# A one-core Perceiver block: softmax weights turned by moves and VectorE, and six steps of a hand-written order placed elsewhere

## The chip, the core and the metric

The kernel runs on one core of a Trainium2 chip. A core has a matrix engine (TensorE, PE in the profile; its weight loads are shown as PEld), a vector engine (VectorE, DVE), an engine for activation functions (ScalarE, ACT), a general engine (GpSimd, POOL) and an engine that here only issues transfers (SyncE, SP; its queue is shown as SPq). Each engine executes its own instructions in order, and they wait for one another by semaphores. Data is worked on in on-chip memory of 128 partitions (SBUF); matrix products land in a second, small memory (PSUM).

The metric is the device time of one execution in microseconds, as the median of several runs.

## What is computed

```python
def reference(x, ctx_1024, ...):
    x = x + _L0_xattn_ref(_layernorm(x), ctx_1024, Wq, bq, Wk, bk, Wv, bv, Wr, br)
    x = x + _L0_attn_ref(_layernorm(x), Wq, Wm, W1, W2, g1, b1, g2, b2)
    x = x + _L0_ffn_ref(_layernorm(x), W, b, ids, weights)

# _L0_xattn_ref: cross attention with cosine features of the keys
    Q, K, V = x @ Wq + bq, y @ Wk + bk, y @ Wv + bv
    K_hat = cos(K @ Wr + br)
    probs = softmax(Q @ K_hat.T)
    return probs @ V
# _L0_attn_ref: linear attention (8 heads) with feat = elu(x @ Wq) + 1, then an MLP
    msg = (feat @ (feat.T @ q) / (feat @ sum(feat))) @ Wm
    x = x + layernorm(msg) * g1 + b1
    x = x + layernorm(relu(msg @ W1) @ W2) * g2 + b2
# _L0_ffn_ref: eight of 32 adapters, summed with weights
    out = x @ sum_k(weights[k] * W[ids[k]]).T + sum_k(weights[k] * b[ids[k]])
```

x is [32, 32, 512] (32 batches of 32 rows), the context y is [32, 257, 512], all in float32. W1 is 512x1024, W2 is 1024x512.

## The kernel before

**Groups.** Four batches of 32 rows make a group of 128 rows, one for each partition; there are eight groups (`NG` = 8), g = 0 to 7. The first half of the groups is 0 to 3.

**The order is written out by hand.** The program is a loop over twelve windows `w` of eight units `u` (L1394 to L1420). In each unit first the steps filed with `ahead` for this place are issued, then the unit's own matrix work, then the steps filed with `at`. A "slot" is 8w + u. Since each engine works in order, this listing is the order on every engine. Within one place, steps stand in the order in which they were filed.

- Windows 0 to 7 make the key features of two batches per four units: `pair_unit`, seven products P1 to P7 of four 128x256 matmuls each (L533), by a scheme that forms sums of blocks first. `ORDER` (L568) is its listing: T1 to T4 are the block sums on VectorE (L521 to L527), C11, C22, C12 and C21 take a product out of PSUM (C22 and C12 are L550 on VectorE, p1, u1, p5 and C21 run on ScalarE, L545), w11 and so on round (ScalarE, L553), f11 and so on take the fraction (VectorE, L557 and L558), S is the sine. A and B turn the next context tiles (L391) and start a later load. P4 adds to the PSUM tile that C22 reads first, and it needs T4; P6 needs T2.
- Windows 8 and 10 are the first MLP product of the first and second half of the groups (`hidden_unit`), by the same scheme with m2 in the place of the context; windows 9 and 11 are the second MLP product (`mlp_unit`).

**A group's steps.** `q_stats`, `q_norm`, `q_turn`, `q_times` make the query; `a_scores` the scores and exp; `a_turn_p` turns the softmax weights p; `a_sum` multiplies them with the plain context (`av`, L828); `a_turn`, `a_values`, `a_norm`, `b_turn`, `b_q`, ... go on to the linear attention; `b_merge` gives m2, `b_turn_m2` writes it turned into `m2T[half]`, from which `m2_sum` makes the block sums t1, t2 and t4 for P5, P6 and P4 of `hidden_unit`. `mlp_stats` and `mlp_norm` norm the MLP's rows; `f_stats`, `f_norm`, `f_turn`, `f_times` are the adapter product. The adapters themselves are summed by 16 `adapter_add` (L718), moved by `adapter_move` and turned by `adapter_turn` into `wff`.

**Two ways to turn a tile.** `turn` (L254) transposes 128x128 blocks on TensorE into PSUM and copies them out. `move` and `turn_moved` (L270, L281) move four blocks of columns with four transfers on SP's queue to 32 partitions each, and transpose 32x32 blocks on VectorE (L283). `a_turn_p` turns p with two TensorE transposes (L817) and a ScalarE copy (L819), behind the unit of step 3; the other turns of groups 0 to 6 are moves. Group 7 (`late`) turns everything on TensorE.

**What shares an engine.** `ln_stats` uses VectorE for statistics and GpSimd for the power (L246, L248); `add_bv` (L761), `mlp_norm` of groups 0 to 3 (L1230, L1231), `f_bias` (L1249) and the sum of two bias rows (L1425) are 128x512 operations on GpSimd.

The lines that file the steps which the change touches:

```python
u = 8 * g + 8 if g < NG - 1 else 8 * g + 4              # q_turn, q_times
steps = {a_scores: 2, a_turn_p: 3, a_sum: 5, ...}       # at
first = {a_turn: 7, a_norm: 9, b_turn: 10, ...}         # ahead
at(0, 4, add_bv, 0)
ahead_slot(slots["add0"] + m, adapter_add, m)
at_slot(slots["m2"], b_turn_m2, NG - 1)                 # slot 79
at_slot(slots["v3" if n else "v1"], m2_sum, 1, i)       # slot 79
```

Of the kernel before, what the change touches and what calls it, by code (L numbers as in the profile page):

```python
# [9 lines left out]
F32 = mybir.dt.float32  # L10
# [16 lines left out]
def tile_perceiver_block(  # L27
# [242 lines left out]
    def move(src, name):  # L270


        m = tmp.tile([P, 4, P], F32, tag="moved", name=f"moved_{name}", bufs=4)
        for q in range(4):
            nc.sync.dma_start(
                out=m[q * 32 : (q + 1) * 32, :, :].rearrange("k n f -> k (n f)"),
                in_=src[:, q * P : (q + 1) * P],
            )
        return m

# [6 lines left out]

    def rows_times(ps, srcT, w):

        n = srcT.shape[1]  # L290
        for c in range(n):
            nc.tensor.matmul(  # L292
                ps, lhsT=srcT[:, c, :], rhs=w[:, c, :], start=(c == 0), stop=(c == n - 1)
            )
# [222 lines left out]

    def block_sum(y11, y12, y21, y22, i):
        t1, t2, t4 = pair_tiles["sums"]
        if i == 1:  # L520
            nc.vector.tensor_tensor(t1, y12, y11, ALU.subtract)  # L521
        elif i == 2:
            nc.vector.tensor_tensor(t2, y22, t1, ALU.subtract)
        elif i == 3:
            nc.vector.tensor_tensor(y12, y22, y12, ALU.subtract)
        else:
            nc.vector.tensor_tensor(t4, y21, t2, ALU.subtract)  # L527
# [264 lines left out]
    def a_scores(g):  # L792
# [17 lines left out]
        nc.vector.reciprocal(rden, den)  # L810
        held["p", g], held["rden", g] = p, rden

    def a_turn_p(g):
        p = held["p", g]
        ps = tr_tile(f"tr_p_{g}")
        for c in range(2):
            nc.tensor.transpose(ps[:, c, :], p[:, c:K0:2], ident)  # L817
        pT = one.tile([P, 2, P], F32, tag="pT", name=f"pT_{g}")
        nc.scalar.copy(pT, ps[:, :2, :])  # L819
        held["pT", g] = pT  # L820
# [222 lines left out]

    def m2_sum(half, i):
        (y11, y12), (y21, y22) = m2_blocks(half)
        block_sum(y11, y12, y21, y22, i)

# [3 lines left out]
    def hidden_unit(half, k, u):  # L1051
# [24 lines left out]
        if u == 0:  # L1076
            product(a, w11, y11, stop=False)
            product(c, w12, y21)
            nc.scalar.copy(part[0], a)
        elif u == 1:  # L1080
            product(a, s2, t2, start=False, stop=False)
            product(d, s1, t1, stop=False)
            add(h[0][0], c, part[0])
            nc.scalar.copy(part[1], a)
            nc.scalar.copy(part[2], d)
        elif u == 2:
            product(a, s3, y12, start=False, stop=False)
# [176 lines left out]

    def f_rows(g, i=0):
        cols = f_parts(g)[i]
# [4 lines left out]
        ff_ps[g, i] = ps[:, : cols.stop - cols.start]  # L1271
        rows_times(ff_ps[g, i], held["h2T", g], ad["wff"][:, :, cols])

# [32 lines left out]

    slots = dict(load3=67, add0=66, wff=83, n=79, f=84, fT=88, ft=89, w1=71, w3=73, w2=66, s0=61, s1=66, t1=63, t3=64, m2=79, v1=79, v3=79, bias=66, h1=72, h2=72, h3=73)
    last = (64, 65, 66, 67, 68, 69, 70, 71, 73, 74, 75, 76, 77, 78, 85, 88)
    six = dict(b_q=10, b_pairs=13, b_msg=14, b_merge=18, b_feat=11, b_turn_f=13, b_turn_msg=16, b_turn_m2=21, b_stats=20, b_norm=21)

    for g in range(NG):
# [3 lines left out]
        if g:  # L1315
            u = 8 * g if g < NG - 1 else 8 * g - 4
            ahead(u // 8, u % 8, q_stats, g)
            ahead((u + 5) // 8, (u + 5) % 8, q_norm, g)
        u = 8 * g + 8 if g < NG - 1 else 8 * g + 4
        ahead(u // 8, u % 8, q_turn, g)  # L1320
        at(u // 8, u % 8, q_times, g)
        w = g + 1
        if g == NG - 1:
# [5 lines left out]
            continue  # L1329
        steps = {a_scores: 2, a_turn_p: 3, a_sum: 5, a_values: 8, b_q: 11, b_pairs: 15, b_msg: 17, b_merge: 22}  # L1330
        first = {a_turn: 7, a_norm: 9, b_turn: 10, b_feat: 13, b_turn_f: 14, b_turn_msg: 20, b_stats: 23, b_norm: 26, b_turn_m2: 31}
        if g == NG - 2:
# [4 lines left out]
        for f, u in first.items():  # L1337
            ahead(w + u // 8, u % 8, f, g)
    at(0, 4, add_bv, 0)
    at(6, 4, adapter_fetch)  # L1340
# [3 lines left out]
    for m in range(2 * NK):  # L1344
        at_slot((59, 60, 63)[m] if m < 3 else slots["load3"] + m - 3, adapter_load, m)
        ahead_slot(slots["add0"] + m, adapter_add, m)
    for c in range(OP):
# [11 lines left out]
    at_slot(slots["ft"] + 1, f_times, 1)  # L1359
    at_slot(slots["m2"], b_turn_m2, NG - 1)  # L1360
    at_slot(68, second_homes)
# [26 lines left out]
    for i in range(1, 5):  # L1388
# [3 lines left out]
        at_slot(slots["t3" if n else "t1"], m2_sum, 0, i)  # L1392
        at_slot(slots["v3" if n else "v1"], m2_sum, 1, i)
    for w in range(12):  # L1394
        for u in range(8):
# [25 lines left out]
            if (w, u) == (0, 2):  # L1421
                add_r = load_row("add_r", b1)
                b2_r = row_tile("b2_r")
                nc.gpsimd.dma_start(out=b2_r, in_=b2.partition_broadcast(P))
                nc.gpsimd.tensor_tensor(add_r, add_r, b2_r, ALU.add)  # L1425
            if (w, u) == (2, 0):
# [19 lines left out]
    f_bias(5)  # L1446
    f_turn(6)
    f_rows(5)
    f_bias(6)
# [61 lines left out]
```

## Time and profile before

| what | value |
|---|---|
| runs before | median 520.6 us of 3 (519.8 to 521.55) |
| the profiled execution | 521.03 us, of it a span of 519.2 us from its first to its last instruction |
| instructions | 9195 |
| granted TensorE clock | 1.000 |
| TensorE / weight loads busy | 511.3 us / 374.2 us |
| VectorE, ScalarE, GpSimd busy | 382.6, 243.9, 164.7 us |
| transfers | 74.64 MB, mean 144 GB/s |
| 436 to 449 us of the span (window 10 begins) | TensorE 11.85, VectorE 12.55, ScalarE 6.41, GpSimd 10.12 us busy in 13.00 |
| 493 to 509 us | TensorE 15.23, VectorE 13.32, GpSimd 6.70 us busy in 16.00 |

The window of group g's scores begins about 44.5 us after that of group g - 1; the eight `a_scores` products start at 65.8, 101.3, 143.5, 188.0, 232.6, 277.2, 321.7 and 358.2 us. A line of the timeline gives start and duration in us, engine, source line, operation, the tiles written and read with partitions x elements, a count, and in brackets the idle time of that engine before it with what ended it. The waits list gives who waited for whom. The chain of waits is followed back from the last instruction.

### The profile page before, as it was taken

What the parts mean: (1) busy time and instruction counts of PE and PEld (TensorE: products, weight loads), DVE (VectorE), ACT (ScalarE), POOL (GpSimd) and SP (SyncE); (2) the same over time, 40 slices, a digit from 0 to 9 for tenths busy, and PEclk for the clock granted to TensorE, in tenths of its full rate; (3) what the DMA queues carried; (4) which work ended last, traced back from release to release, by engine and by line L of the source; (5) the groups of instructions that cost most, each with busy time, mean ns of one, the idle gap of its engine ahead of it and who ended that gap; (6) DMA issues with size and microseconds to landing.
All of it is one profiled execution on the core that took longest, in us unless ns stands there. A gap on an engine that the chain in (4) does not pass through costs nothing.

```text
span 519.2 us, 9195 instructions
## 1 busy us (share of the span) xinstructions
PE 511.3 (98%) x3413; PEld 374.2 (72%) x3413; DVE 382.6 (74%) x645; ACT 243.9 (47%) x465; POOL 164.7 (32%) x202
## 2 busy tenths in 40 slices
PE   8999999999999999999999999999999999999997
PEld 6588977777866767687676778866576786886844
DVE  1398877787886978878779778667476977875593
ACT  1145684485474467348446646735332222451131
POOL 0012110500501340250144316203415836973134
PEclk9999999999999999999999999999999999999999
DMA  8759987655455547824544372535344433211013
GB/s 206 165 126 214 276 181 222 169 151 165 149 168 153 160 124 176 240 77 136 166 146 138 98 228 63 164 103 189 127 152 163 161 101 126 77 56 52 20 41 123
DMA packets 84517, 74.64 MB, mean 144 GB/s; under 512 B 7972, under 2 KB 70448, under 8 KB 84472
## 3 DMA queue, kind: packets, MB, share of 16 engines
q1 hardware_dynamic: 81312, 64.19, 44.6%
q0 software_dynamic: 2864, 9.73, 6.1%
q8 instruction: 27, 0.44, 0.4%
q14 instruction: 18, 0.15, 0.1%
q10 hardware_dynamic: 296, 0.14, 0.1%
HBM read 58.03 MB, written 2.10 MB: 116 GB/s over the span
## 4 chain that ended last, share of the span: by engine, by line
PE 88%; DVE 5%; DMA 2%; POOL 2%; issue 1%; ACT 1%; SPq 1%; POOLq 0%; DVEq 0%; ACTq 0%
PE a L533 20%; PE b L533 9%; PE q L779 6%; PE bq L292 5%; PE xa L292 5%; PE c L533 5%; PE m L292 5%; PE hid_a L533 5%; PE ff L292 3%; PE wkr L324 3%; PE av L828 3%; PE mlp_a L1169 3%; PE sc L797 3%; PE mlp_b L1169 2%; PE hid_b L533 2%; PE z L429 2%
## 5 line engine op out<-in xcount | busy, mean ns | idle before, releaser
L557 DVE SCALAR_TENSOR_TENSOR kh<-parts,kh 128x512 f32<-128x512 f32 x60 | 42.7, 712 | 24.9 <-ACT parts L553 24.9
L553 ACT ACTIVATE parts<-kh,rounder 128x512 f32<-128x512 f32 x60 | 43.2, 720 | 35.8 <-DVE kh L550 35.3
L566 ACT ACTIVATE kh<-kh 128x512 f32<-128x512 f32 x60 | 36.3, 628 | 34.9 <-DVE kh L558 34.6
L246 POOL TENSOR_TENSOR rstd_n<-ve_n,mhalf 128x1 f32<-128x1 f32 x16 | 12.1, 758 | 97.8 <-DVE ve_n L244 96.7
L391 DVE STREAM_TRANSPOSE yT<-quads 128x1024 f32<-128x1024 f32 x31 | 38.2, 1234 | 2.2 <-DMA quads<-in_ctx_dram 2.2
L558 DVE TENSOR_SCALAR kh<-kh 128x512 f32<-128x512 f32 x60 | 31.5, 524 | 2.1
L246 POOL TENSOR_TENSOR rstd_x<-ve_x,mhalf 128x1 f32<-128x1 f32 x8 | 7.7, 962 | 77.8 <-DVE ve_x L244 77.8
L779 PEld LDWEIGHTS q<-hT,wq_sb 128*128 128x128 f32 x256 | 29.8, 192 | 3.1 <-issue 2.6
L533 PE MATMUL a<-sums,wkr 128*128 128x256 f32 x120 | 29.2, 386 | 1.7 <-DVE kh L550 1.7
L779 PE MATMUL q<-hT,wq_sb 128*128 128x128 f32 x256 | 29.9, 275 | 0.0
L533 PE MATMUL a<-yT,m2T 128*128 128x256 f32 x120 | 29.6, 389 | 0.0
L533 PEld LDWEIGHTS a<-sums,wkr 128*128 128x128 f32 x120 | 22.1, 190 | 9.9 <-issue 4.0
L761 POOL TENSOR_TENSOR x<-x,bv_r 128x512 f32<-128x512 f32 x8 | 10.7, 1331 | 57.6 <-ACT h L252 57.6
L533 PE MATMUL a<-yT,wkr 128*128 128x256 f32 x120 | 28.9, 384 | 0.0
L292 PE MATMUL ff<-awq_sb,h2T 128*128 128x512 f32 (+2 forms) x80 | 28.6, 508 | 0.2 <-DVE h2T L283 0.2
L292 PE MATMUL xa<-wv_sb,aoT 128*128 128x512 f32 x64 | 28.8, 592 | 0.0
L292 PE MATMUL bq<-awq_sb,bhT 128*128 128x512 f32 x64 | 28.8, 592 | 0.0
L292 PE MATMUL m<-awm_sb,msgT 128*128 128x512 f32 x64 | 28.8, 592 | 0.0
L533 PE MATMUL a<-sums,m2T 128*128 128x256 f32 x120 | 28.4, 379 | 0.0
L533 PE MATMUL c<-yT,wkr 128*128 128x256 f32 x120 | 28.3, 379 | 0.0
L533 PE MATMUL b<-sums,m2T 128*128 128x256 f32 x120 | 28.3, 379 | 0.0
L533 PE MATMUL b<-yT,m2T 128*128 128x256 f32 x120 | 28.3, 379 | 0.0
(274 smaller groups left out, 1138.8 us busy)
## 6 DMA issues: line engine op xcount, KB each, us to landing
quads<-in_ctx_dram SPq DMA_DIRECT2D x128, 128.0 KB, 3.1
plain<-in_ctx_dram SPq DMA_DIRECT2D x32, 512.0 KB, 5.5
moved_h<-h SPq DMA_DIRECT2D x56, 64.0 KB, 2.2
x<-in_x_dram SPq DMA_DIRECT2D x8, 256.0 KB, 4.4
last<-in_ctx_dram SPq DMA_DIRECT2D x32, 64.0 KB, 2.2
w<-in_L_attn_W_dram SPq DMA_DIRECT2D x4, 512.0 KB, 4.5
moved_ao<-ao SPq DMA_DIRECT2D x28, 64.0 KB, 2.2
moved_bh<-bh SPq DMA_DIRECT2D x28, 64.0 KB, 2.2
```

What stands on the lines that cost most here:

```text
L246: nc.gpsimd.tensor_tensor(rstd, ve, mhalf, ALU.pow)
L292: nc.tensor.matmul(ps, lhsT=srcT[:, c, :], rhs=w[:, c, :], start=(c == 0), stop=(c == n - 1))
L324: nc.tensor.matmul(acc[c], lhsT=wkT[:, e, c * P : (c + 1) * P], rhs=wr_sb[:, e, :], start=(e == 0), stop=(e == DC - 1),)
L391: nc.vector.transpose(t.rearrange("p c (n k) -> p n c k", k=32), quads.pop(b))
L533: nc.tensor.matmul(ps[:, o, :], lhsT=w[:, c, o * P : (o + 1) * P], rhs=yb[:, c, :], start=start and o == 0 and c == 0, stop=stop and o == ...
L553: nc.scalar.activation(w, u, AF.Identity, bias=rounder)
L557: nc.vector.scalar_tensor_tensor(u, w, ROUNDER, u, ALU.subtract, ALU.subtract)
L558: nc.vector.tensor_scalar(u, u, -0.5, 0.5, ALU.max, ALU.min)
L566: nc.scalar.activation(u, u, AF.Sin, scale=-TURN)
L779: nc.tensor.matmul(ps[:, e, :], lhsT=wq_sb[:, d, e * P : (e + 1) * P], rhs=hT[:, d, :], start=(d == 0), stop=(d == DC - 1),)
L797: nc.tensor.matmul(sc[js, :], lhsT=qT[g][:, r, js], rhs=kh[g * GB + j][:, r, :], start=(r == 0), stop=(r == DC - 1),)
L1169: nc.tensor.matmul(ps[:, o, :], lhsT=a[n // 2][:, n % 2, o * P : (o + 1) * P], rhs=b[n // 2][:, n % 2, :], start=start and o == 0 and n == ...
```

## The change

1. `a_turn_p` of groups 0 to 6: `a_scores` now moves the first 256 columns of p with four transfers (`move` takes any width), and `a_turn_p` is one VectorE transpose from the moved tile; it is filed ahead of step 5 and not behind step 3. Group 7 keeps the TensorE way.
2. `add_bv(0)` goes from place (0, 4) to (1, 0), the sum of the two bias rows from (0, 2) to (0, 6); `q_turn` and `q_times` of group 0 go one unit later; `b_turn` of group 0 is filed behind its unit's own work and not ahead of it.
3. `b_turn_m2(7)` goes from behind slot 79 into slot 80, between the first and the second product. The sums t1 and t2 of the second half are made in two column halves: groups 4 and 6 at slot 79, groups 5 and 7 behind `b_turn_m2(7)`. The other two sums (`v3`) go to slot 80.
4. The last two `adapter_add` go one slot later. `mlp_stats` and `mlp_norm` of groups 0 to 3 go two slots later, `f_stats`, `f_norm`, `f_turn` and `f_times` (of 0 and 1) one.
5. In the tail, `f_turn(6)` stands between the first and the second matmul of `f_rows(5)`, and not in front of them.

```diff
     def move(src, name):
-        m = tmp.tile([P, 4, P], F32, tag="moved", name=f"moved_{name}", bufs=4)
+        n = src.shape[1] // 4
+        m = tmp.tile([P, 4 * n], F32, tag="moved", name=f"moved_{name}", bufs=4)
         for q in range(4):
             nc.sync.dma_start(
-                out=m[q * 32 : (q + 1) * 32, :, :].rearrange("k n f -> k (n f)"),
-                in_=src[:, q * P : (q + 1) * P],
+                out=m[q * 32 : (q + 1) * 32, :], in_=src[:, q * n : (q + 1) * n]
             )
-        return m
+        return m.rearrange("p (n f) -> p n f", n=4)
...
-    def rows_times(ps, srcT, w):
+    def rows_times(ps, srcT, w, between=None):
         n = srcT.shape[1]
         for c in range(n):
+            if c == 1 and between:
+                between()
...
-    def block_sum(y11, y12, y21, y22, i):
-        t1, t2, t4 = pair_tiles["sums"]
+    def block_sum(y11, y12, y21, y22, i, cols=slice(0, 2 * P)):
+        y11, y12, y21, y22, t1, t2, t4 = (
+            t[:, :, cols] for t in (y11, y12, y21, y22, *pair_tiles["sums"])
+        )
...
         held["p", g], held["rden", g] = p, rden
+        if not late(g):
+            held["pm", g] = move(p[:, :K0], f"p_{g}")

     def a_turn_p(g):
-        p = held["p", g]
-        ps = tr_tile(f"tr_p_{g}")
-        for c in range(2):
-            nc.tensor.transpose(ps[:, c, :], p[:, c:K0:2], ident)
         pT = one.tile([P, 2, P], F32, tag="pT", name=f"pT_{g}")
-        nc.scalar.copy(pT, ps[:, :2, :])
+        if late(g):
+            p = held["p", g]
+            ps = tr_tile(f"tr_p_{g}")
+            for c in range(2):
+                nc.tensor.transpose(ps[:, c, :], p[:, c:K0:2], ident)
+            nc.scalar.copy(pT, ps[:, :2, :])
+        else:
+            nc.vector.transpose(
+                pT.rearrange("p c (k n) -> p n c k", n=4),
+                held.pop(("pm", g)).rearrange("p n (i c) -> p n c i", c=2),
+            )
         held["pT", g] = pT
...
         if u == 0:
             product(a, w11, y11, stop=False)
+            if (half, k) == (1, 0):
+                b_turn_m2(NG - 1)
+                m2_sum(1, 1, slice(P, 2 * P))
+                m2_sum(1, 2, slice(P, 2 * P))
             product(c, w12, y21)
             nc.scalar.copy(part[0], a)
...
-    slots = dict(..., n=79, f=84, fT=88, ft=89, ..., v1=79, v3=79, ...)
+    slots = dict(..., n=81, f=85, fT=89, ft=90, ..., v1=79, v3=80, ...)
...
-        u = 8 * g + 8 if g < NG - 1 else 8 * g + 4
+        u = 8 * g + (8 if g < NG - 1 else 4) + (g == 0)
...
-        steps = {a_scores: 2, a_turn_p: 3, a_sum: 5, ...}
-        first = {a_turn: 7, ...}
+        steps = {a_scores: 2, a_sum: 5, ...}
+        first = {a_turn_p: 5, a_turn: 7, ...}
...
         for f, u in first.items():
-            ahead(w + u // 8, u % 8, f, g)
-    at(0, 4, add_bv, 0)
+            (at if g == 0 and f == b_turn else ahead)(w + u // 8, u % 8, f, g)
+    at(1, 0, add_bv, 0)
...
-        ahead_slot(slots["add0"] + m, adapter_add, m)
+        ahead_slot(slots["add0"] + m + (m >= 2 * NK - 2), adapter_add, m)
...
-    at_slot(slots["m2"], b_turn_m2, NG - 1)
...
-        at_slot(slots["v3" if n else "v1"], m2_sum, 1, i)
+        if n:
+            at_slot(slots["v3"], m2_sum, 1, i)
+        else:
+            at_slot(slots["v1"], m2_sum, 1, i, slice(0, P))
...
+            if (w, u) == (0, 6):
                 nc.gpsimd.tensor_tensor(add_r, add_r, b2_r, ALU.add)
...
-    f_turn(6)
-    f_rows(5)
+    f_rows(5, between=lambda: f_turn(6))
```

More of the change, by code (lines that the diff above doesn't have):

```diff
@@ L1042, in m2_blocks, with m2_sum @@
         ]
-    def m2_sum(half, i):
+    def m2_sum(half, i, cols=slice(0, 2 * P)):
         (y11, y12), (y21, y22) = m2_blocks(half)
-        block_sum(y11, y12, y21, y22, i)
+        block_sum(y11, y12, y21, y22, i, cols)
     def hidden_tile(half, i):
@@ L1263, in f_parts, with f_rows @@
         return last if g == NG - 1 else (slice(0, D),)
-    def f_rows(g, i=0):
+    def f_rows(g, i=0, between=None):
         cols = f_parts(g)[i]
@@ L1271, in f_rows @@
         ff_ps[g, i] = ps[:, : cols.stop - cols.start]
-        rows_times(ff_ps[g, i], held["h2T", g], ad["wff"][:, :, cols])
+        rows_times(ff_ps[g, i], held["h2T", g], ad["wff"][:, :, cols], between)
     def f_out(g, i=0):
@@ L1305, in ahead_slot @@
         ahead(n // 8, n % 8, *args)
-    slots = dict(load3=67, add0=66, wff=83, n=79, f=84, fT=88, ft=89, w1=71, w3=73, w2=66, s0=61, s1=66, t1=63, t3=64, m2=79, v1=79, v3=79, bias=66, h1=72, h2=72, h3=73)
+    slots = dict(load3=67, add0=66, wff=83, n=81, f=85, fT=89, ft=90, w1=71, w3=73, w2=66, s0=61, s1=66, t1=63, t3=64, m2=79, v1=79, v3=80, bias=66, h1=72, h2=72, h3=73)
     last = (64, 65, 66, 67, 68, 69, 70, 71, 73, 74, 75, 76, 77, 78, 85, 88)
@@ L1329, in tile_perceiver_block @@
             continue
-        steps = {a_scores: 2, a_turn_p: 3, a_sum: 5, a_values: 8, b_q: 11, b_pairs: 15, b_msg: 17, b_merge: 22}
-        first = {a_turn: 7, a_norm: 9, b_turn: 10, b_feat: 13, b_turn_f: 14, b_turn_msg: 20, b_stats: 23, b_norm: 26, b_turn_m2: 31}
+        steps = {a_scores: 2, a_sum: 5, a_values: 8, b_q: 11, b_pairs: 15, b_msg: 17, b_merge: 22}
+        first = {a_turn_p: 5, a_turn: 7, a_norm: 9, b_turn: 10, b_feat: 13, b_turn_f: 14, b_turn_msg: 20, b_stats: 23, b_norm: 26, b_turn_m2: 31}
         if g == NG - 2:
```

## The prediction

> **What bounds the kernel now.** I read first the page's busy times, then what TensorE waited for in the whole run, then the chain of waits and the timelines around each stall.
>
> ```profile
> PE 511.3 (98%) x3413; PEld 374.2 (72%) x3413; DVE 382.6 (74%) x645; ACT 243.9 (47%) x465; POOL 164.7 (32%) x202
> ...
> PE 88%; DVE 5%; DMA 2%; POOL 2%; issue 1%; ACT 1%; SPq 1%; POOLq 0%; DVEq 0%; ACTq 0%
> ```
>
> TensorE is busy for 98% of the span and carries 88% of the chain, at a granted clock of 1.0 throughout. So a microsecond is won only by taking work off TensorE or by closing one of its gaps. This is the complete list of its gaps with a releaser (line, releaser: us in total, times, longest):
>
> ```profile
> PE a L533 <- DVE kh L550: 1.7, 2, 1.0
> PE idle L308 <- POOL ident masks.py:199: 1.4, 1, 1.4
> PE tr_m L258 <- ACT m2s L969: 0.7, 1, 0.7
> PE tr_h L258 <- ACT h L252: 0.6, 1, 0.6
> PE hid_a L533 <- DVE hid L1073: 0.4, 1, 0.4
> PE ff L292 <- DVE h2T L283: 0.2, 1, 0.2
> ```
>
> Without the start-up (L308) that is 3.6 us. The change touches the place of each of them except the last.
>
> **A. Softmax weights turned without TensorE.** For groups 0 to 6 two transposes a group leave TensorE (group 7 keeps them). Their price is the hole that they leave in the chain of waits between bq and the next product:
>
> ```profile
> 191.84 3.43 PE bq L292 x8
> ...
> 195.51 1.73 PE a L533 x8
> ```
>
> bq ends at 195.27, the product starts at 195.51: 0.24 us. The same reading gives 0.23 or 0.24 in each of the seven groups: 7 x 0.235 = 1.65 us won. ScalarE loses seven copies of 0.38, which end nothing. Added are, per group, four 32 KB moves on SP's queue and one VectorE transpose of 128x256 in front of T3. No row shows either. I bound the transpose from below by a quarter of the 128x1024 one (1.24/4 = 0.31) and from above by the whole 128x512 one of `turn_moved` (1.10); half of the latter, 0.55, has the same scattered output and is my value. A 64 KB move lands 2.2 us after issue (median; 2.1 to 4.0 over all moved_h rows), and its issues are 0.6 apart. In group 3's window of the timeline (T3, the product with the weights, f11):
>
> ```profile
> 197.81 0.68 DVE L525 TENSOR_TENSOR yT<-yT 128x512 f32<-128x512 f32 x1
> ...
> 202.35 1.92 PE L828 MATMUL av<-plain,pT 128*32 128x512 f32 x16
> ...
> 203.16 0.69 DVE L557 SCALAR_TENSOR_TENSOR kh<-parts,kh 128x512 f32<-128x512 f32 x1 [1.65 <-ACT parts L553]
> ```
>
> The softmax is done at 192.4, SP has issued its quads by 194.4 (192.51 and 1.86); the fourth move goes at 196.2 and lands at 198.4. VectorE comes to it at 197.81, so it waits 0.6 and is done at 199.0 (0.31: 198.7; 1.10: 199.5). TensorE needs pT at 202.1: 3.1 us of slack. T3, C11, T4 and A behind it slip by 1.2 us, and the 1.65 us in which VectorE then waits for ScalarE takes that up. On SP the x and W loads and the moved f (197.92, needed at 205.25) slip by up to 2.4 and 1.0 us, within what they have. Price 0. Without that cover, 1.2 us a window would meet C22 and P4: 7 x 1.2 = 8.4 us. Group 0 is tighter: DMA share is 1.01 from 60 to 70 us and quads land 3.7 us after issue, but av (76.77) still leaves some 2 us.
>
> The Trainium skill speaks against this part twice. "VectorE: DVE Perf Modes", Rules for kernel authors, gives a 128x128 transpose to TensorE where PSUM will do; by it A would be worth nothing and the sum below 1.65 us less. The rows above, TensorE full and VectorE idle behind it, decide otherwise. "DMA: Bandwidth & Descriptors", Specifications, asks for at least 512 B a piece, and the new pieces are 256 B (64 floats); no row isolates that size, and a move twice as slow would still land in the slack and leave the sum alone.
>
> **B. First keys.** The timeline before the first of the two L550 waits:
>
> ```profile
> 46.92 1.27 POOL L761 TENSOR_TENSOR x<-x,bv_r 128x512 f32<-128x512 f32 x1
> ...
> 47.26 1.48 DVE L557 SCALAR_TENSOR_TENSOR kh<-parts,kh 128x512 f32<-128x512 f32 x1
> ```
>
> f11 takes 1.48 beside GpSimd's x add and 0.69 elsewhere (203.16 above), so C22 starts 0.79 late, at 49.11, and P4 (49.85) waits 0.75. With `add_bv(0)` behind step (1,0) that add falls near 58, and C22 would end at about 49.0, when P3 does (49.11): 0.72 won. The `add_r` sum keeps its time, since it waits for its DMA until 45.44; only the kh copies pass it, and behind the x add on GpSimd's queue nothing comes before 67.75. The earlier stream would then reach q at 54.6 with hT done at 55.02 - which is why the order of q and its turn matters: one step later, hT (1.14 us) goes in front of T3 and q's 3.57 us behind P5, at 58; VectorE is then done with hT near 57.5. Scores follow at 65, qT needs 1.14 after 61.5. Price 0; if hT slips, 0.3.
>
> **C. Group 0's bh turn.** bhT waits 2.47 us for its move at 102.38 and holds C22 (103.48); P4 stalls 0.96. Behind step (2,2) C22 can go at 99.95, B, C12 and T1 fill VectorE until 103.1, the move has landed at 102.3, and bhT is done at 104.2, before bq (105.2). Queued behind it is group 1's maximum, which ran at 106.39 and now runs sooner. 0.96 won.
>
> **D. Into the last MLP half.** 436 to 449 us holds 12.55 us of VectorE work in 13.0, so VectorE sets this stretch. m ends at 436.04. Now P1 follows (437.77), then tr_m (438.2; ScalarE's copy ends 439.1), P2 (439.95). The half-width T1 and T2 of group 7 take 0.4 each (a 128x256 product row is 0.38): 439.9, just in time for P6. Group 6's halves run before, under the wait; four halves cost 1.5 against 1.36 for two whole. Then VectorE does T3, T4 (0.60 each), adapter sum 14 (1.2), h00 (0.6), two statistics (2.0), sum 15 (1.2) and h11 (0.68): 6.9 us to 446.8. TensorE does P6, P5, P7, P3 in 6.92, to 446.87. P4 can then start near 446.9 to 448.0 (one sum stretched by GpSimd, as acc was to 2.29 at 441.49), against 448.4 before. 0.5 to 1.5, I take 1.1. The moves of the adapter's rows follow their sums, which now end at 442.3 and 446.1 against 443.8 and 447.1; their 16 issues keep their place on SP. Norms 0 to 3 and their GpSimd products (1.28 each, two a group) go some 6 us later; at 3.4 us of GpSimd a group from 444 (0.55, 0.26 and two 1.28) x3 is complete near 460, and h of group 0 leaves ScalarE near 458 as before. ff moves one step back; its h2T had 4.3 us of slack (464.7 to 468.99), and the wait for the fourth h2T falls in VectorE's 5.27 us of idleness before 486.7. Each f_norm's four moves and f_times' one store find SP free (its 14 h issues from 458.7 took 11.8 us). Price 0.
>
> **E. Tail.** The timeline of the last two norms and the turn between them:
>
> ```profile
> 503.94 0.81 ACT L252 ACTIVATE h<-x,shift_h,rstd_h 128x512 f32<-128x512 f32 x1 [2.98 <-POOL shift_h L248]
> ...
> 504.81 0.66 PE L258 MATMUL tr_h<-ident,h 128*128 128x128 f32 x4 [0.60 <-ACT h L252]
> ...
> 507.54 0.81 ACT L252 ACTIVATE h<-x,shift_h,rstd_h 128x512 f32<-128x512 f32 x1 [2.79 <-POOL shift_h L248]
> ```
>
> ff5's first quarter (0.86) covers the wait for h6, but h7 is ready at 508.35 whatever TensorE does (VectorE is full from 490.4 to 506.4), so the second turn now waits: the last 6.96 us start at 508.87 and not 509.34. 0.45 won, 0 to 0.6.
>
> **Sum.** 1.65 + 0.72 + 0.96 + 1.1 + 0.45 = 4.88 us off the profiled execution's 521.03 (span 519.2 and 1.83 around it): 516.15. That execution lies 0.43 above the median of the runs, 520.6, so the same sum gives 515.7 there. I forecast 516.0, between the two. Bounds of the terms: 1.65, 0.4 to 0.75, 0.7 to 0.96, 0.5 to 1.5, 0 to 0.6, together 3.25 to 5.5, so its own range is 515.1 to 517.8.
>
> **Rivals.**
> 1. The gaps only move: TensorE's work shrinks by 1.65, but VectorE's full stretch (436 to 449) and tail give back D and E, and B or C meets the next late operand. For it: the 12.55 of 13.0, and q at 55.30, which had 0.2 us to spare. Against: C22 in C has 3 us of room. 520.6 - 1.65 - 0.5 = 518.4. Chance 0.17.
> 2. Slower: the moved p lands late in VectorE's queue. Slack in group 3 is 3.1 us beyond a landing of 2.2, so it starts at 5.3 us; from there each us costs 7 us over the groups, and at 6.0 the 4.9 us are gone. With 6.6 (as W's quarters near 69 us) it gives 7 x 1.3 = 9.1 back: 524.8. For it: pieces of half the usual size, 28 more issues. Against: moves of as many pieces land in 2.2. Chance 0.05.
> 3. The change does not do what it says: the stalls have other causes (f11 not slowed by GpSimd), and pT's turn eats the hole on TensorE: 520.6, chance 0.05.
>
> The forecast has 0.73. A change under 0.3% (1.56 us) can't be told from none. Faster: 0.73 + nearly all of rival 1 (0.14) = 0.87; the rest of rival 1 and rival 3, 0.08, is no change; slower 0.05. The range for 8 in 10 runs from 514.9 to 518.8, into rival 1.
>
> **What would show it.** A: no tr_p before group 7, bq followed at once by the product, pT before av by over 1 us. B and C: the L550 rows gone from TensorE's waits. D: no tr_m wait, P4's wait under 1.1. E: tr_h waiting below 0.6, once for h7. Wrong: TensorE waiting at av for a transpose, or at q for hT.

## The result, and the profile after

| | before | changed |
|---|---|---|
| median of 7 runs each | 520.63 us (519.8 to 521.58) | 517.19 us (515.91 to 518.36) |
| ratio to before | | 0.9927, 95% interval 0.9916 to 0.9939 |
| the profiled execution | 521.03 us, span 519.2 | 516.95 us, span 515.2 |
| instructions | 9195 | 9223 |
| packets under 512 B | 7972 | 12004 |

The change makes the kernel 3.44 us faster on the medians and 4.08 us between the two profiled executions. The forecast was 516.0 us and, term by term, 4.88 us less.

The first view is the page of the changed kernel, its busy times and its chain of waits:

```profile
PE 509.2 (99%) x3399; PEld 372.1 (72%) x3399; DVE 386.1 (75%) x654; ACT 242.0 (47%) x458; POOL 162.1 (31%) x202
...
PE 90%; DVE 5%; DMA 2%; ACT 1%; SPq 1%; issue 1%; POOL 0%; DVEq 0%; POOLq 0%
```

TensorE has 14 instructions and 2.1 us less, VectorE 3.5 us more. The second view is all that TensorE of the changed kernel waited for (the code has moved by a few lines: L550 before is L554 here, L533 is L537, L545 is L549):

```profile
PE idle L310 <- POOL ident masks.py:199: 1.4, 1, 1.4
PE a L537 <- ACT parts L549: 0.7, 1, 0.7
PE a L537 <- DVE kh L554: 0.3, 1, 0.3
PE ff L294 <- DVE h2T L283: 0.3, 1, 0.3
PE tr_h L258 <- ACT h L252: 0.2, 1, 0.2
```

Without the start-up 3.6 us of gaps have become 1.5. The waits for m2, for `hid` and one of the two for `kh` are gone, that for h has shrunk, and a wait for ScalarE's `parts` (0.7) is new.

To see where the time came from I cut both profiled executions at starts of the same TensorE work, all read from the timeline, and took differences:

| stretch | before | changed | won | forecast |
|---|---|---|---|---|
| start of the span to P7 of the first block | 45.48 | 44.94 | 0.54 | 0 |
| that P7 to the scores of group 0 | 20.28 | 20.86 | -0.58 | B 0.72 |
| scores of group 0 to scores of group 1 | 35.54 | 35.31 | 0.23 | A, first group |
| scores of group 1 to bq of group 0 | 4.74 | 3.71 | 1.03 | C 0.96 |
| bq of group 0 to scores of group 7 | 252.03 | 250.51 | 1.52 | A, six groups; A in all 1.65 |
| scores of group 7 to P4 of the last MLP half | 90.31 | 88.96 | 1.35 | D 1.1 |
| P4 to the MLP's last quarter (mlp_b) | 34.60 | 34.49 | 0.11 | 0 |
| mlp_b to the last 32 matmuls | 26.19 | 26.04 | 0.15 | E 0.45 |
| these to the end of the span | 10.03 | 10.38 | -0.35 | 0 |
| sum | 519.2 | 515.2 | 4.0 | 4.88 |

A, C and D hold. B does not show in this pair, and E came to a third. The first row is a difference that the change does not make: it is how much the first 45 us, in which the weights and the first context tiles are loaded, differ between two executions. In the 14 profiles of this study that P7 starts between 44.50 and 45.48 us. The last row comes back below, in the part on the prediction.

**A.** In the chain of waits bq is followed at once by the product; there is no hole of 0.24 left:

```profile
190.20 3.43 PE bq L294 x8
193.63 1.73 PE a L537 x8
```

The timeline of group 3 shows the turn that took its place (start, duration; in brackets the idle time before it):

```profile
197.14 0.65 DVE L829 STREAM_TRANSPOSE pT<-moved_p 128x256 f32<-128x256 f32 x1 [0.70 <-DMA moved_p<-p]
...
200.47 1.07 PE L841 MATMUL av<-plain,pT 128*32 128x512 f32 x8
```

VectorE waits 0.70 for the moved p (forecast 0.6), the transpose takes 0.65 (median of the seven 0.656, forecast 0.55), and pT is there at 197.79, 2.7 us before av (forecast 3.1).

**B.** The turn of context tile 5 before, in the profile that the prediction used:

```profile
49.76 1.25 DVE L391 STREAM_TRANSPOSE yT<-quads 128x1024 f32<-128x1024 f32 x1
```

The timeline of the first window of the changed kernel:

```profile
47.09 0.65 DVE L561 SCALAR_TENSOR_TENSOR kh<-parts,kh 128x512 f32<-128x512 f32 x1
...
50.13 1.25 DVE L393 STREAM_TRANSPOSE yT<-quads 128x1024 f32<-128x1024 f32 x1 [1.34 <-DMA quads<-in_ctx_dram]
51.30 0.65 DVE L554 SCALAR_TENSOR_TENSOR kh<-b,parts 128x512 f32<-128x512 f32 x1
...
54.97 1.99 PE L537 MATMUL a<-sums,m2T 128*128 128x256 f32 x8 [0.68 <-ACT parts L549]
```

f11 is short without GpSimd beside it, 0.65 and not 1.48, just as the forecast had it. "GPSIMD Engine Reference", Specifications, in the Trainium skill, says that GpSimd shares its SBUF interfaces with VectorE and that VectorE's instructions with two SBUF inputs contend; f11 has two, and the pair of durations agrees. But then the turn of context tile 5 (50.13) waits 1.34 us for its transfer, where the row of before shows no wait. Behind it C12 and w12 are late, ScalarE reaches the second block's first part late, and P6 waits 0.68 for it.

**C.** Before, the turn of bh of group 0 waited for its move, and P4 of that unit for C22 behind it:

```profile
102.38 1.25 DVE L283 STREAM_TRANSPOSE bhT<-moved_bh 128x512 f32<-128x512 f32 x1 [2.47 <-DMA moved_bh<-bh]
...
104.21 1.99 PE L533 MATMUL a<-sums,wkr 128*128 128x256 f32 x8 [0.96 <-DVE kh L550]
```

Now the turn does not wait and stands behind T1, and P4 follows the scores at once:

```profile
102.58 1.12 DVE L283 STREAM_TRANSPOSE bhT<-moved_bh 128x512 f32<-128x512 f32 x1
...
102.99 1.99 PE L537 MATMUL a<-sums,wkr 128*128 128x256 f32 x8
104.82 3.60 PE L294 MATMUL bq<-awq_sb,bhT 128*128 128x512 f32 x8
```

**D.** Before, TensorE waited in front of the turn of m2 and at P4:

```profile
436.92 0.66 PE L258 MATMUL tr_m<-ident,m2s 128*128 128x128 f32 x4 [0.72 <-ACT m2s L969]
...
448.38 1.99 PE L533 MATMUL hid_a<-sums,w 128*128 128x256 f32 x8 [0.43 <-DVE hid L1073]
```

Now the last MLP half runs without a gap from P1 to P4; TensorE is the bound of this stretch, not VectorE:

```profile
433.29 1.89 PE L537 MATMUL hid_a<-m2T,w 128*128 128x256 f32 x8
435.02 0.60 PE L258 MATMUL tr_m<-ident,m2s 128*128 128x128 f32 x4
435.46 1.89 PE L537 MATMUL hid_c<-m2T,w 128*128 128x256 f32 x8
...
444.29 1.89 PE L537 MATMUL hid_a<-sums,w 128*128 128x256 f32 x8
```

**E.** The wait for h6 is covered by the first quarter of the product; the turn of h7 waits 0.22 in its stead, as forecast, and the product two steps earlier waits 0.28 for its h2T where it waited 0.17.

### The profile page after: what moved, and what is told of

Same layout as the page of the kernel before. It is cut to its first block, busy times and chain, and to the rows that moved or that the text cites. A ratio compares the mean times of both kernels' runs of the same rounds, so it can differ in the third digit from the quotient of the medians.

```text
span 515.2 us, 9223 instructions
## 1 busy us (share of the span) xinstructions
PE 509.2 (99%) x3399; PEld 372.1 (72%) x3399; DVE 386.1 (75%) x654; ACT 242.0 (47%) x458; POOL 162.1 (31%) x202
## 2 busy tenths in 40 slices
DMA packets 88550, 75.57 MB, mean 147 GB/s; under 512 B 12004, under 2 KB 74480, under 8 KB 88504
## 4 chain that ended last, share of the span: by engine, by line
PE 90%; DVE 5%; DMA 2%; ACT 1%; SPq 1%; issue 1%; POOL 0%; DVEq 0%; POOLq 0%
PE a L537 19%; PE b L537 9%; PE q L783 6%; PE hid_a L537 6%; PE m L294 5%; PE bq L294 5%; PE xa L294 5%; PE c L537 4%; PE mlp_a L1187 3%; PE sc L801 3%; PE av L841 3%; PE wkr L326 3%; PE mlp_b L1187 3%; PE ff L294 3%; PE hid_b L537 3%; PE mlp_c L1187 2%
## 5 line engine op out<-in xcount | busy, mean ns | idle before, releaser
L537 PE MATMUL a<-yT,m2T 128*128 128x256 f32 x120 | 29.6, 389 | 0.0
L537 PE MATMUL a<-sums,wkr 128*128 128x256 f32 x120 | 29.2, 386 | 0.3 <-DVE kh L554 0.3
L537 PE MATMUL a<-sums,m2T 128*128 128x256 f32 x120 | 28.5, 380 | 0.7 <-ACT parts L549 0.7
L537 PE MATMUL a<-yT,wkr 128*128 128x256 f32 x120 | 28.9, 383 | 0.0
L537 PE MATMUL b<-sums,m2T 128*128 128x256 f32 x120 | 28.3, 379 | 0.0
L537 PE MATMUL b<-yT,m2T 128*128 128x256 f32 x120 | 28.3, 379 | 0.0
L537 PE MATMUL c<-yT,wkr 128*128 128x256 f32 x120 | 28.3, 379 | 0.0
L537 PEld LDWEIGHTS a<-sums,wkr 128*128 128x128 f32 x120 | 22.1, 190 | 8.4 <-issue 4.0
```

The lines of the kernel that those rows point to most:

```text
L537: nc.tensor.matmul(ps[:, o, :], lhsT=w[:, c, o * P : (o + 1) * P], rhs=yb[:, c, :], start=start and o == 0 and c == 0, stop=stop and o == ...
```

## Experiments

The edits are against the changed kernel unless it says otherwise. Intervals are 95%.

| kernel | median us | ratio to before |
|---|---|---|
| changed, again (4 runs) | 516.2 | 0.9912 (0.9897 to 0.9926) |
| before, again (1 run) | 520.26 | |
| A undone | 518.02 | 0.9950 (0.9937 to 0.9962) |
| before with B alone | 519.94 | 0.9993 (0.9983 to 1.0003) |
| q of group 0 back | 516.32 | 0.9928 (0.9913 to 0.9942) |
| value weights at units 6 to 8 | 518.02 | 0.9953 (0.9937 to 0.9969) |
| value weights at 9 to 12, query weights at 13 to 16 | 515.22 | 0.9906 (0.9890 to 0.9923) |
| the same, and q back | 515.69 | 0.9905 (0.9890 to 0.9919) |
| last sums and first norms back | 521.07 | 1.0003 (0.9989 to 1.0016) |
| m2's turn and sums back | 517.07 | 0.9940 (0.9923 to 0.9957) |
| tail's turn of h6 back | 518.0 | 0.9951 (0.9932 to 0.9969) |
| weights later, h7's turn inside too | 516.11 | 0.9914 (0.9901 to 0.9927) |

Runs of one kernel spread over some 2 us (up to 3.5), so terms of some tenths are read from the stretches of the profiles and not from these times.

### A undone

```diff
-        if not late(g):
-            held["pm", g] = move(p[:, :K0], f"p_{g}")
...
-        steps = {a_scores: 2, a_sum: 5, ...}
-        first = {a_turn_p: 5, a_turn: 7, ...}
+        steps = {a_scores: 2, a_turn_p: 3, a_sum: 5, ...}
+        first = {a_turn: 7, ...}
```

> The changed kernel with part A undone (p of groups 0 to 6 turned by TensorE again). Theory: the turn by moves is worth the seven holes and nothing hides it, so this is 1.65 us above the changed kernel's 517.2: 518.8, and the chain of waits again has 0.23 to 0.24 us between bq's end and the product in each group. Rival 1 (part A costs something elsewhere, in the crowded transfers of the first 100 us): the first group's scores and av come earlier than with A, and the whole is under 1 us above, 517.2 to 518.2. Rival 2 (the hole is filled by other waits anyway): 517.2.

The hole is back in the chain of waits of this kernel:

```profile
190.44 3.43 PE bq L294 x8
193.87 0.24 PE tr_p L823 x2
194.11 1.73 PE a L537 x8
```

From the scores of group 0 to those of group 1 it takes 35.54 again (changed 35.31), from bq of group 0 to the scores of group 7 251.93 (250.51): 0.23 + 1.42 = 1.65 us. That this meets the forecast to the hundredth is luck, the size is not: over all profiles the second stretch takes 250.42 to 250.77 in the ten with A and 251.93 to 252.27 in the four without, 1.43 apart on the means. The median, 518.02, is only 0.83 above that of the changed kernel and not the 1.65 of the theory; it lies where rival 1 had it, and the first window was shorter in the profile (scores of group 0 at 65.40 against 65.80), which is how rival 1 was worded. But that window ends before the first move of p goes (68.95 in the changed kernel), and the next experiments show that it differs from execution to execution without A. Rival 2 falls.

### B alone, and its parts

Before with B alone:

```diff
-        u = 8 * g + 8 if g < NG - 1 else 8 * g + 4
+        u = 8 * g + (8 if g < NG - 1 else 4) + (g == 0)
...
-    at(0, 4, add_bv, 0)
+    at(1, 0, add_bv, 0)
...
+            if (w, u) == (0, 6):
                 nc.gpsimd.tensor_tensor(add_r, add_r, b2_r, ALU.add)
```

> The kernel before with part B alone (both adds later on GpSimd, q and its turn of group 0 one unit later). Forecast on record: 0.72 us less than before, 519.9. Theory now: f11 falls to 0.65 us and the product P4 waits 0.3 instead of 0.75, but the move of q takes away the work that covered P6's wait for ScalarE's part, which shows as a new wait of 0.6 to 0.7 us, so that the scores of group 0 start at 65.8 as before: 520.6, within 0.3. Rival (the first window is bound by the landing of the context tiles, and it varies from run to run): the two waits differ by more than 0.3 from those in the changed kernel.

Then the changed kernel with q back at its old unit:

```diff
-        u = 8 * g + (8 if g < NG - 1 else 4) + (g == 0)
+        u = 8 * g + (8 if g < NG - 1 else 4)
```

> The changed kernel with q and its turn of group 0 back at their old unit, between P2 and P6; both adds stay late. If the loss of the cover is what ate part B, the wait of P6 for ScalarE (0.7 us) goes and q waits 0.3 at most for hT: the scores of group 0 start at 65.2 to 65.5 instead of 65.87, and the time is 516.5 to 516.9. Rival (VectorE's chain is late because of the context tile that lands late, whatever stands in between): q waits for hT, or P6 still waits, the scores start at 65.8 or later, 517.2 or above.

And both kernels once more:

> The changed kernel once more, for a second profile of its first window. Theory (part B is worth what the landing of context tile 5 leaves of it, and that differs from execution to execution): the turn of tile 5 starts at 49.0 to 50.2 and the scores of group 0 at 64.9 to 65.8, most likely near 65.1 as in three of the five profiles with this window; everything behind the scores keeps its distances within 0.1: scores of group 1 to bq 3.7, m(7) to P4 14.6. Rival (the loss of part B is fixed, 65.80 in each execution): 65.7 to 65.9 again. Time 516.5 to 517.5.

> The kernel before once more, one look. Theory: with f11 stretched beside GpSimd, the stall in front of P4 is set by VectorE and not by the landing, so the scores of group 0 start at 65.6 to 65.9 again. Rival (the landing shifts this kernel too): more than 0.3 off 65.76.

Since the start of the first block shifts by itself, the first window is measured from its P7 to the scores of group 0. `kh` and `parts` are TensorE's waits at P4 and P6 in between, "tile 5" is how long after that P7 the turn of context tile 5 starts:

| kernel | P7 to scores | wait at P4 | wait at P6 | tile 5 | from there to the scores |
|---|---|---|---|---|---|
| before | 20.28 | 0.75 | 0 | 4.28, no wait | 16.00 |
| before, again | 20.66 | 0.91 | 0 | 4.65, waits 0.17 | 16.01 |
| before with B alone | 19.83 | 0 | 0.16 | 4.16, waits 0.82 | 15.67 |
| changed | 20.86 | 0.29 | 0.68 | 5.19, waits 1.34 | 15.67 |
| changed, again | 20.55 | 0 | 0.60 | 4.88, waits 1.26 | 15.67 |
| A undone | 20.29 | 0 | 0.36 | 4.63, waits 1.02 | 15.66 |
| last sums and norms back | 20.49 | 0 | 0.52 | 4.83, waits 1.19 | 15.66 |
| m2's turn back | 20.35 | 0 | 0.42 | 4.68, waits 1.09 | 15.67 |
| tail's turn back | 20.19 | 0 | 0.29 | 4.53, waits 0.96 | 15.66 |
| q back | 20.07 | 0 | 0, but 0.58 at q for hT | 4.10, waits 0.79 | 15.97 |

The seven rows with all of B have 20.37 on the mean, the two without it 20.47, and one execution differs from the next by up to 1.0: these means cannot price B. The last column can. Once the turn of tile 5 starts, the scores follow 15.66 or 15.67 us later in all seven profiles with B, 16.00 and 16.01 without it, 15.97 with q back. So for the same landing of tile 5, B is worth 0.33 us, not 0.72; 0.30 of it is the later place of q, and the two adds by themselves leave 0.03. The rest of the first column is when tile 5 lands, and among the seven rows with B the wait at P6 and the start of tile 5 rise together, row by row. So what bounds this window is the landing of tile 5. The median of B alone, 0.55 us below that of before beside it (520.49), agrees, but its interval (0.9 us less to 0.2 more) would not exclude 0.72.

Both expectations of a fixed loss fall: B alone had its 0.45 in this one profile (no wait of 0.6 at P6), and the kernel before was 0.38 longer the second time. With q back the scores start at 64.94 and the time is 516.32, both below what was expected; q waits 0.58 for hT, more than the 0.3 expected, and the early scores are an early landing (4.10). My first theory, that moving q took away P6's cover and lost B's gain, had it the wrong way round: q waits longer at its old place than P6 does at the same landing, and the move won 0.30.

One row of the kernel before hid this.

```profile
49.15 1.25 DVE L391 STREAM_TRANSPOSE yT<-quads 128x1024 f32<-128x1024 f32 x1 [0.17 <-DMA quads<-in_ctx_dram]
```

That is the turn of tile 5 in its second profile, where it waits 0.17. In the first, at 49.76, it showed no wait because it stood behind C22, which GpSimd had made late. It had no room even so: the semaphore of the last of its four transfers rises for the last time at 49.57 in that trace, and in the nine profiles in which the turn waits it starts 0.19 or 0.20 us behind that rise, as it does here.

### Loads out of the way of the context tiles

If the landing bounds the window, then loads that share the DMA engines with the tiles do. From 40 to 60 us the mean DMA share is 1.04 to 1.14 in the changed kernel, and the value weights (4 x 256 KB, first used at 87 us) are issued at 37.84 and 44.60. First they go to units 6 to 8:

```diff
-    at_units = (2, 3, 4, 4, 9, 10, 11, 12, 18, ...)
+    at_units = (6, 7, 8, 8, 9, 10, 11, 12, 18, ...)
```

> The changed kernel with the four loads of the value weights from units 2, 3, 4, 4 to units 6, 7, 8, 8, out of the stretch from 37 to 47 us in which transfers keep the DMA engines full. If late context tiles set this stretch, the turn of the tile for keys 5 (1.34 us of waiting for its transfer at 50.1) waits under 0.3, P4's 0.29 and P6's 0.67 us go, and the time is 516.2 to 516.5. Rival (ScalarE's own stream sets P6): the transfer wait goes and P6's stays, 516.9 to 517.2. Rival 2 (the loads collide with the moves of p and h from 65 us on instead): the waits go, but av of group 0 waits, 517.2 or more.

P7 to scores takes 19.21, with no wait in TensorE, and the turn of tile 5 does not wait. But the timeline further on shows what my second rival said:

```profile
75.90 0.64 DVE L829 STREAM_TRANSPOSE pT<-moved_p 128x256 f32<-128x256 f32 x1 [4.61 <-DMA moved_p<-p]
...
76.58 1.92 PE L841 MATMUL av<-plain,pT 128*32 128x512 f32 x16 [1.61 <-DVE pT L829]
```

The loads have moved in front of the first moves of p on SP's queue: p is issued at 71.95 where it went at 68.95, VectorE waits 4.61 us for it, and av 1.61. Scores of group 0 to scores of group 1 take 37.90 instead of 35.31: 1.65 won, 2.59 lost. This is the mechanism of the prediction's slower rival, provoked in group 0. Next the value weights take the places of the query weights, and these go behind them:

```diff
-    at_units = (2, 3, 4, 4, 9, 10, 11, 12, 18, ...)
+    at_units = (9, 10, 11, 12, 13, 14, 15, 16, 18, ...)
```

> The changed kernel with the four quarters of the value weights filed behind units 9 to 12 (where the query weights of the linear attention went) and those behind units 13 to 16. Theory: the first window is bound by the landing of context tiles 4 and 5 in full DMA engines, so without these loads from 37 to 47 us both waits of TensorE go and the scores of group 0 start at 64.2, as in the run with the loads at units 6 to 8; and since SP's queue is no fuller at the moves of p than in the changed kernel, av of group 0 doesn't wait: 515.4 to 515.8. Rival 1: the moves of p land late again (av waits 1 us or more): 516.8 to 517.5. Rival 2: the later query weights reach bq of group 0 or the moves behind it late: a new wait there, 517 or more.

All that TensorE of this kernel waits for:

```profile
PE idle L310 <- POOL ident masks.py:199: 1.4, 1, 1.4
PE ff L294 <- DVE h2T L283: 0.3, 1, 0.3
PE tr_h L258 <- ACT h L252: 0.2, 1, 0.2
```

And tile 5 is turned at once behind C22:

```profile
47.63 1.23 DVE L393 STREAM_TRANSPOSE yT<-quads 128x1024 f32<-128x1024 f32 x1
```

P7 to scores is 19.20, scores to scores 35.31, av does not wait. The median is 515.22. With q back as well:

> As the kernel before in this list, with q and its turn of group 0 at their old unit. Theory: where the context tiles land in time, the place of q decides nothing more; the scores of group 0 start at 64.2 and the time is within 0.3 of that kernel. Rival (q's place is worth something by itself, through the turn of h in front of VectorE's T3): a wait of q for hT of 0.3 or more, or scores that start 0.3 or more off.

P7 to scores is 19.21 again: where the tiles land in time, q's place decides nothing. The scores themselves start 0.67 later than in the kernel above and the median is 0.47 higher, both outside the expected 0.3; the first block's P7 already started 0.66 later. In all four kernels with later loads this stretch is 19.20 or 19.21, where it varied by 1.0 before. So B's part is settled: its idea was right for 0.33 us, and 1.17 us (20.37 - 19.20) lay behind the landing. The later loads were not run on the kernel before, so whether they need B's adds stays open.

### D in two halves

The last two adapter sums and the first norms back, the turn of m2 stays:

```diff
-        ahead_slot(slots["add0"] + m + (m >= 2 * NK - 2), adapter_add, m)
+        ahead_slot(slots["add0"] + m, adapter_add, m)
...
-    slots = dict(..., n=81, f=85, fT=89, ft=90, ...)
+    slots = dict(..., n=79, f=84, fT=88, ft=89, ...)
```

> The changed kernel with the last two adapter sums and the first MLP norms at their old places; the turn of m2 and the half-width sums stay. Theory: m(7) to P4 of the last half, 11.0 us in the changed kernel and 12.34 before, takes 11.4 to 11.8, since two statistics and a sum of VectorE come back in front of T4: 517.6 to 518.0. Rival (the gap of that stretch was tr_m and the sums alone): still 11.0, 517.2.

A miss of both theories. From the scores of group 7 to P4 takes 95.50 and not 88.96. The timeline of TensorE:

```profile
434.63 1.89 PE L537 MATMUL hid_c<-m2T,w 128*128 128x256 f32 x8
440.18 3.75 PE L537 MATMUL hid_a<-sums,wq_sb 128*128 128x256 f32 x8 [3.65 <-DVE sums L527]
443.73 3.00 PE L537 MATMUL hid_b<-sums,wq_sb 128*128 128x256 f32 x8
```

and of VectorE:

```profile
436.08 0.41 DVE L525 TENSOR_TENSOR sums<-m2T 128x256 f32<-128x256 f32 x1
...
436.87 1.28 DVE L722 SCALAR_TENSOR_TENSOR acc<-adapter,w_r,acc 128x1024 f32<-128x1024 f32 x1
...
438.52 1.52 DVE L527 TENSOR_TENSOR sums<-m2T,sums 128x256 f32<-128x256 f32 x1
```

The second column halves of T1 and T2 are now filed inside the unit, so two statistics (2.0 us), filed at slot 79, and an adapter sum (1.28), filed ahead of the unit, stand in front of them, and T2's second half is stretched from 0.42 to 1.52 as GpSimd works on the first norms beside it. P6 waits 3.65 us. Then TensorE is slow on top: the next 16 matmuls take 6.4 us instead of 3.5. The profiled execution, 522.71 us, is one of the two slowest of twelve; by the medians this kernel is 0.4 us slower than the one before run beside it (521.07 against 520.71).

m2's turn and the whole sums at slot 79 again, sums and norms stay later:

```diff
-            if (half, k) == (1, 0):
-                b_turn_m2(NG - 1)
-                m2_sum(1, 1, slice(P, 2 * P))
-                m2_sum(1, 2, slice(P, 2 * P))
...
+    at_slot(slots["m2"], b_turn_m2, NG - 1)
...
-        if n:
-            at_slot(slots["v3"], m2_sum, 1, i)
-        else:
-            at_slot(slots["v1"], m2_sum, 1, i, slice(0, P))
+        at_slot(slots["v3" if n else "v1"], m2_sum, 1, i)
```

> The changed kernel with the turn of m2 of group 7 and the sums t1 and t2 at their old places and width; adapter sums and norms stay later. Theory: TensorE waits 0.7 for m2 in front of tr_m again, and P6 for T2 not at all or little: m(7) to P4 takes 11.7 to 12.3 instead of 11.0, 517.9 to 518.5. Rival (later sums and norms alone free VectorE, and the wait at tr_m moves elsewhere): 11.0 to 11.2, 517.2 to 517.4.

TensorE waits 0.72 at tr_m again, and scores of group 7 to P4 takes 89.70: 0.74 more than changed. The median, 517.07, lies below both expectations. A nearer mark than these scores is the start of group 7's product m, since in the second profile of the changed kernel 1.06 us are lost between the two, outside D (90.02 from the scores). From m to P4 takes 14.43 in all nine profiles with the whole of D and 15.17 here. In the three with the old order (with B alone among them) it took 15.77, 15.17 and 15.93; in the second, the kernel before once more, P4 does not wait for `hid`. So of D's 0.74 to 1.50 us the turn of m2 inside the unit is worth 0.74 and the later sums and norms 0 to 0.76, by execution. The halves do not add up: the first alone took 5.2 us more than before in its profile (95.50 - 90.31), the slow clock included, since it puts the sums behind what the second takes away.

### E, and one step further

```diff
-    f_rows(5, between=lambda: f_turn(6))
+    f_turn(6)
+    f_rows(5)
```

> The changed kernel with the turn of h of group 6 in front of the tail's product again. From the last quarter of the MLP (mlp_b) to the last 32 matmuls took 26.03 us before and 25.87 in the changed kernel. Theory: it is 26.0 to 26.1 again, so the part is worth 0.16 and not the forecast's 0.45, since the wait moves to the turn of group 7 (0.2) and the product in front of it (0.3): 517.3. Rival (the forecast's 0.45 is there and another part takes it back): 26.3.

The two numbers on record for before and changed, 26.03 and 25.87, set the chain's start of mlp_b against the timeline's start of the last matmuls. Read like that this kernel has 26.16; by the timeline alone it is 26.19 before, 26.04 changed and 26.32 here. Undoing E costs 0.28, less than the forecast's 0.45, more than the 0.15 against before; the h2T wait of 0.30, 0.13 more than before, is the difference.

The same trick for h7, on top of the later loads:

```diff
-    f_turn(7)
-    f_rows(6)
+    f_rows(6, between=lambda: f_turn(7))
```

> The changed kernel with the value and query weights later, as in the run with 515.2 us, and the turn of h of group 7 also between the first and the second matmul of its neighbour's product. Theory: the wait of 0.22 in front of that turn goes under the first matmul, so the last 32 matmuls start 0.2 earlier behind mlp_b (25.7) and nothing waits behind them: 515.0, and 1.5 to 2 us under the changed kernel run beside it. Rival (the last product then waits for the copy of h of group 7, 0.59): no gain or 0.2 lost against 515.2.

```profile
503.50 1.12 PE L294 MATMUL ff<-awq_sb,h2T 128*128 128x512 f32 x2 [0.69 <-ACT h2T L259]
504.46 0.60 PE L258 MATMUL tr_h<-ident,h 128*128 128x128 f32 x4
```

It does not pay. The wait of 0.22 is gone, but that transposition had itself stood between the turn of h6 and the product that reads it; without it the product waits 0.69 for ScalarE's copy. From mlp_b to the end takes 36.83 us against 36.39 without this edit.

## Why the prediction was right, and where it was not

**A** is right as reckoned: seven holes of 0.235, 1.65 us by undoing it. Its transpose was valued at 0.55 and took 0.656, the landing 2.2 and took 2.4 at the median, the slack at av 3.1 and was 2.7; none of these reached the sum. The cover that it leans on is real, as the 2.59 us lost by loads in front of the first moves shows. What it priced at 0 and is not: the end of the span, see below.

**B** is the step that failed. "C22 would end at about 49.0" held within 0.3, and so did f11's cause; "the earlier stream would then reach q at 54.6" did not. The term of 0.72 measures 0.33 for the same landing of tile 5, almost all of it from the place of q, which the prediction priced at 0; in the profiled pair it is -0.58, since the tile landed later. I had read the row of tile 5 at 49.76, which shows no wait, as an operand with room; it had none. Rival 1's clause, that B or C "meets the next late operand", is what happened to B alone, and its reason for it (q at 55.30) was the wrong one.

**C**: 0.96 forecast, 1.03 measured. bhT was forecast to be done at 104.2, just before bq; it was done at 103.70, and the stall was gone. No run undoes C alone; the stretch takes 4.48 to 4.74 in the three profiles with the old order and 3.70 or 3.71 in the eleven with the new.

**D**: 1.1 forecast, 1.35 between the profiles, 0.74 to 1.50 over all. The end that I left out of my own value was GpSimd's stretch of an adapter sum: I allowed for one, and none came, since the norms that caused it went later (both sums take 1.28 and 1.27). That the turn of m2 would ruin the stretch without the later norms is not in the prediction.

**E**: 0.45 forecast, 0.15 to 0.28 measured. That h7 waits was reckoned; that the product before h6's turn would wait 0.28 for its h2T instead of 0.17 was not.

The end of the span, 0.35 longer behind the last matmuls' start, was not forecast. 0.24 of it lies behind VectorE's last operation: the span ends 2.84 us after it and not 2.60. The last store does not land later (1.56 and 1.57 us after that operation); but behind that landing SyncE has seven waits for semaphores left where it had three, at 0.06 us each. The ten profiles with A end 2.83 to 2.85 us after VectorE, the four without it, with A undone among them, 2.60. So A brings this 0.24, and its net is 1.4 us; why A leaves more of these waits behind the landing is not shown.

The terms as measured, 1.65 + 0.33 + 1.03 + 1.35 + 0.15 - 0.24, make 4.3 us, against 4.88 forecast, 3.44 between the medians and 4.08 between the profiled executions. The time was 1.2 us above the 516.0 of the forecast in the first seven runs and 0.2 above in the four run later; a landing of tile 5 some tenths earlier or later moves it as much as B does.

Rival 2, the moves of p landing late, cost nothing in the changed kernel: two moves of group 6 took 6.56 and 5.77 us, past the 5.3 at which it starts, but pT was there 4.0 us before av even so. Rival 3 is excluded by f11's 0.65 and by the chain of A.

One variant is better than the kernel before by more than the change: value and query weights later, 515.22 and, with q back, 515.69 us. That it also beats the changed kernel is supported by the first window, 1.17 us shorter and free of TensorE waits in each of the four profiles with later loads; the intervals of the ratios, 0.9890 to 0.9923 against 0.9916 to 0.9939, overlap, so the times alone do not settle it.

## What to carry to other kernels

An operation that shows no wait in a profile had its data in time, not with room to spare: before counting on starting it earlier, ask when its transfer landed, and take a second profile if it can be had. Where whole stretches vary from execution to execution, measure from the event that varies (here the turn of tile 5): behind it the distances repeated within 0.01 us. Where a window is bound by landing, move a load that is not yet needed, and look at which moves on the same queue it now precedes. Parts of one change that share an engine's queue can depend on each other; measure one without the other before calling either good or bad.

## What was not expected of the hardware

**A short stall costs TensorE its clock.** In the kernel with sums and norms back, the granted clock by stretches (busy time, clock, DMA share, GB/s) was:

```profile
440.20:443.70 3.50, 3.50 (x8) 0.50 0.34 100
443.70:446.50 2.80, 2.80 (x9) 0.60 0.19 53
446.50:450.00 3.50, 3.50 (x18) 1.00 0.27 77
```

After 3.65 us of waiting the clock is 0.50, and eight matmuls that take 1.73 us take 3.55. By the mean of 0.60 in the second stretch, the full clock is back only near 446, some 5.8 us after the matmuls began again. Asked in narrower stretches, the profile has 1.00 from 436.60 to 439.10, 0.50 from 439.20 to 445.90 and 1.00 from 446.00: the clock fell 2.6 us after the last matmul before the wait had ended (436.52) and stayed low for 6.8. "TensorE: Matmul & The Clock Gate", Part 1: The HAM clock gate, in the Trainium skill, has half rate after at least one idle window of about 3.4 us and full rate after at least one such busy one, with windows that run on by themselves. The halving agrees, but it came after less than 3.4 us without matmuls, and the recovery took longer; windows that did not begin with the wait could explain both, which is not shown.

The loss differs from run to run: of this kernel's twelve, four have a mean clock of 0.999 or 1.000 over the whole span and took 519.30 to 520.83 us, seven have 0.996 or 0.997 (520.54 to 522.84), and the profiled one 0.993. None of the shorter waits in these profiles, up to 1.61 us, shows it. Where in between it begins is not measured; of the six runs of the kernel with the 1.61, the slowest (519.44) has a mean clock of 0.997.

**Landing times shift by a microsecond.** The same four transfers of one context tile are turned 4.5 to 5.2 us after the same matmul in the six profiles with all of B and the changed kernel's loads (the rows above from 'changed' to 'tail's turn back'). The DMA share is near 1.1 there. How much of the spread between runs comes from this is not shown: the kernels with later loads, in which the window is fixed at 19.20 or 19.21, still spread over 0.9 to 2.8 us.
